# Triangle multiplication and a Fourier layer on one Trainium2 core: transposed sides kept one step apart, and the transform's sums moved to ScalarE's queue with two buffers

## The chip, the cores and the metric

The kernel runs on one core of one Trainium2 chip, as a single program. The metric is device time in microseconds. Of the kernel before there are three timed runs: 1973.91, 1974.03 and 1977.88 us, so the median is 1974.03 us. The engines have short names in what follows: PE is TensorE (matmuls and transposes), DVE is VectorE, ACT is ScalarE, POOL is GpSimd, and SP is SyncE, which only starts transfers. An engine followed by q (SPq, ACTq) means the transfers that this engine starts.

## The reference, cut to what matters

The input is one image of 512 × 512 positions with 64 channels, float32. Two layers follow each other, and each is added to its input.

```python
# layer 0: triangle multiplication on the group-normed input
xn = layernorm(gn(x))
left  = (xn @ left_w  + left_b)  * mask * sigmoid(xn @ lgate_w + lgate_b)
right = (xn @ right_w + right_b) * mask * sigmoid(xn @ rgate_w + rgate_b)
out_gate = sigmoid(xn @ ogate_w + ogate_b)
out = einsum('bkjd,bkid->bijd', left, right)       # per channel a 512 x 512 x 512 product
x = x + (layernorm(out) @ out_w + out_b) * out_gate

# layer 1: spectral convolution on the group-normed result
x_ft = fft2(gn(x))[..., :12, :12]                  # 12 x 12 modes are kept
x = x + real(ifft2(einsum('bcmn,comn->bomn', x_ft, w_real + 1j * w_imag)))
```

The mask is the product of a 0/1 vector over rows with the same over columns, so whole rows and columns of left and right are zero. Only the rows whose mask is 1 take part in the product.

## The kernel before, in words

The program counts the rows whose mask is 1 and takes a compact branch when there are at most 256, which is the case measured. There the triangle's sides are 256 × 256 for each of the 64 channels. The output rows without the mask get the bias of the output projection alone in the place of the triangle's result.

Four stages follow each other: the group norm's statistics and the gathering of the masked rows (0 to some 225 us), the projections to left and right (to some 440 us, written to the tensors `left_d` and `right_d` in device memory), the joint stage (to some 1660 us), and the inverse transform with the output (to 1973 us). The change lies in the joint stage.

The joint stage is one software-pipelined loop over steps `s`; a unit `k` has 8 steps, and `n` is the step within the unit. A unit is 256 rows by 32 columns of the image, and holds two blocks of 128 rows. There are 40 units: units 0 to 13 are rows without the mask (half 1) of the first 14 column groups, units 14 to 21 are the rows of the triangle's products (LayerNorm and output projection, stored to `u_d`), unit 22 (called `first`) and unit 39 (called `last`) are the two remaining groups without the mask, and units 23 to 38 are the masked rows (half 0) of all 16 column groups. All engines get their instructions in the order of the Python loop: it runs under a manual schedule, so the order inside a step is the order on each engine.

What the steps do, by the names in the code:

- **Sides** (`load_side`, `turn_side`, `keep_side`). Each of the 128 sides (64 channels, left and right) is loaded by SP into one of four `loose` buffers, transposed by PE (L1147) into `side_ps`, of which there is one PSUM buffer, and copied to one of four `turned_sides`. A left side is copied half by DVE (L1158) and half by ACT (L1159). A right side is copied and masked by two ACT operations (L1156).
- **Triangle** (`triangle`, `masked`). Each half of a channel's product is two matmuls on PE (L1167) into one half of the single PSUM tile `tri_pair`. DVE masks it one step later (L1174) into `staged`; after the second half SP stores the channel to `tri_d`. `halves` gives the steps of the 128 halves: two in each of the 12 steps before step 0, then 104 of them spread over steps 0 to 93, so most steps there hold one and a few hold two.
- **Rows of the image** (`transpose`, `centered`, `squared`, `summed`, `root`). PE transposes the rows (L992), multiplies them by the centring weights (`y_ps`, L1015, in the first units together with the gate's weights; `c_ps`, L999, from unit 22 on), ACT squares the result (L1035), DVE sums the squares (L1046), and once a unit, at n = 5, ACT takes the root (L1052).
- **Gate** (`gated`, `added`, `load_u`). The projection is scaled on DVE (L1333, L1339), passed through the sigmoid on ACT (L1275), multiplied on POOL by the triangle's result `u` (L1074) and added on POOL to the image rows (L1078). Four quarters `c` of a unit follow each other in this way, each of them over two steps. In units 23 to 38 the rows of `u` come through `load_u`: 32 transfers on SP (L1065), one for each of 32 columns, whose row number is read from registers that SP loads first (L646). Even quarters need the transfers 0 to 15, odd ones 16 to 31. There are two buffers for `u`.
- **Transform** (`transform`, `save`, `fetch`, `columns`). At n = 0 and n = 4 of the following unit, PE multiplies the two row blocks of a finished unit by the row basis (L1108) into `f_ps`. At n = 5 ACT copies it (L1119) into the buffer `ft`, and four transfers of 48 KB (L1133) take it to `modes_d`. Seven of the eight transfers that fetch these sums back, 768 KB in most cases, go over SP at n = 6 of certain units (L903) and one over ACT; PE multiplies what was fetched by the column basis (`columns`, L893), and DVE adds it to `sums` (L897).
- **Stores of rows** (`store`). SP stores each finished row block to `x1_h` (L1094), the first at n = 7 of the unit and the second at n = 3 of the next.

The order inside a step of the loop is this: transposes of later rows, `masked` of the half that the step before left, the projection, `centered`, `transform`, then for each half `triangle` and the transposes `turn_next` of the side two halves later, then on ACT the sigmoid, `root`, `squared`, then `keep_next` of the side just transposed, `save`, POOL's `gated` or `added`, and DVE's statistics, sums and scaling. Line numbers in this text are those of the kernel before.

## Time and profile before

The numbers are of one profiled execution, with its own time beside its span.

| | value |
|---|---|
| median of three runs | 1974.03 us (1973.91 to 1977.88) |
| profiled execution, its own time | 1974.68 us |
| its span, from first to last instruction | 1972.9 us |
| mean granted clock of TensorE in it | 0.852 |
| PE busy | 1588.0 us, 80% of the span |
| PE weight loads busy | 1217.3 us, 62% |
| DVE busy | 1412.6 us, 72% |
| ACT busy | 1018.8 us, 52% |
| POOL busy | 935.3 us, 47% |
| traffic | 524.41 MB, 266 GB/s over the span |

The page's shares are means over stages that have different limits, so a reader should not add up savings of them. Some lines of the profile give a start, a duration, an engine and a line of the code, then the operation, what it writes and reads and how many it groups, and in brackets how long the engine sat idle before it and what ended that. A list of waits gives, for an engine and a line, what it waited for: the total, how many times, and the longest, in microseconds. Matmuls are pipelined, so that the spans of neighbouring groups on PE overlap.

### The profile page before, as it was taken

How to read it: one execution, taken by the hardware profiler on the slowest of the kernel's cores; microseconds unless marked ns; L12 is line 12 of the kernel's file. 1: busy time of each engine (PE TensorE's matmuls, PEld its weight loads, DVE VectorE, ACT ScalarE, POOL GpSimd, SP SyncE). 2: the span in 40 equal slices, each digit the busy share in tenths (PEclk: the TensorE clock that was granted, in tenths of full speed). 3: DMA queues.
4: the chain of work that ended last, by engine and by line, in shares of the span. 5: the costliest groups of instructions: out<-in, count | busy, mean ns of one | idle time of the engine just before them, and what ended most of it. 6: DMA issues, size and time to landing. Idle time of an engine off the chain costs nothing. (4 is left out here: it accounts for less than half of the span.)

```text
span 1972.9 us, 33265 instructions
## 1 busy us (share of the span) xinstructions
PE 1588.0 (80%) x11014; PEld 1217.3 (62%) x11014; DVE 1412.6 (72%) x2988; ACT 1018.8 (52%) x1853; POOL 935.3 (47%) x695
## 2 busy tenths in 40 slices
PE   6788899976887778877868798788869866998773
PEld 6676666625766656656647697777768753665441
DVE  7989688872467666767798688677768766775552
ACT  3565666643676666656766576565655642111000
POOL 4665111101165455555577688677776756121110
PEclk9989999997999898989879899888989886555555
DMA  7998388877566656656469976776777679999999
GB/s 296 385 386 318 84 240 227 235 235 259 165 226 197 207 184 215 218 186 221 155 170 309 319 251 221 231 233 216 240 256 231 223 226 355 424 427 426 427 427 386
DMA packets 229956, 524.41 MB, mean 266 GB/s; under 512 B 49968, under 2 KB 165936, under 8 KB 188816
## 3 DMA queue, kind: packets, MB, share of 16 engines
q1 hardware_dynamic: 193472, 301.55, 45.1%
q0 software_dynamic: 32832, 218.45, 30.6%
q10 hardware_dynamic: 3472, 2.20, 0.4%
q8 instruction: 90, 1.47, 0.3%
q14 instruction: 90, 0.74, 0.1%
HBM read 314.55 MB, written 207.55 MB: 265 GB/s over the span
## 5 line engine op out<-in xcount | busy, mean ns | idle before, releaser
L1078 POOL TENSOR_TENSOR places<-places,z_t 128x1024 f32<-128x1024 f32 x127 | 299.9, 2362 | 8.2
L1074 POOL TENSOR_TENSOR z_t<-z_t,bias_row_out 128x1024 f32<-128x1024 f32 x63 | 148.7, 2361 | 296.2 <-ACT z_t L1275 194.4
L1503 PE MATMUL l_ps<-places,rinv 24*128 24x512 f32 x512 | 208.2, 1116 | 31.4 <-DVE places L1510 20.1
L1184 DVE BATCH_NORM_STATS2 stats2c<-places 128x6 f32<-128x128 f32 x1024 | 220.5, 279 | 13.4 <-POOL places L1078 13.3
L1046 DVE TENSOR_REDUCE scratch<-sq_c 128x16 f32<-128x1024 f32 x160 | 194.7, 1217 | 47.5 <-ACT sq_c L1035 33.8
L1167 PE MATMUL tri_c_ps<-places 128*128 128x256 f32 x512 | 154.5, 428 | 77.5 <-DVE places L1174 74.2
L1074 POOL TENSOR_TENSOR z_t<-z_t,places 128x1024 f32<-128x1024 f32 x64 | 151.1, 2362 | 115.6 <-ACT z_t L1275 55.7
L999 PE MATMUL c_ps<-center_x,xt_c 128*128 128x128 f32 x1152 | 164.4, 289 | 44.6 <-ACT xt_c L994 43.9
L1503 PEld LDWEIGHTS l_ps<-places,rinv 24*128 24x128 f32 x512 | 120.2, 301 | 114.3 <-DVE places L1510 61.0
L999 PEld LDWEIGHTS c_ps<-center_x,xt_c 128*128 128x128 f32 x1152 | 150.4, 204 | 47.7 <-ACT xt_c L994 46.8
L992 PE MATMUL t_ps<-c_ident,places 128*128 128x128 f32 x1024 | 170.5, 294 | 6.6 <-DMA places<-in_x,src_i 6.6
L999 PE MATMUL w_ps<-gate_x,xt_c 128*128 128x128 f32 x1152 | 166.7, 292 | 11.1 <-DVE z_t L1333 10.7
L1275 ACT ACTIVATE z_t<-z_t 128x1024 f32<-128x1024 f32 x128 | 135.3, 1058 | 67.2 <-DVE z_t L1339 66.0
L1167 PEld LDWEIGHTS tri_c_ps<-places 128*128 128x128 f32 x512 | 92.6, 201 | 119.4 <-DVE places L1174 85.6
L999 PEld LDWEIGHTS w_ps<-gate_x,xt_c 128*128 128x128 f32 x1152 | 152.7, 207 | 18.7 <-DVE z_t L1333 18.7
L1339 DVE TENSOR_TENSOR z_t<-z_t,scratch 128x1024 f32<-128x1024 f32 x128 | 156.3, 1221 | 9.2 <-ACT rs_n L1052 4.0
L688 DVE BATCH_NORM_STATS2 stats1c<-x_ps 128x6 f32<-128x512 f32 x256 | 156.3, 686 | 8.1 <-PE x_ps L687 7.8
L1158 DVE COPY places<-side_ps 128x256 f32<-128x256 f32 x64 | 27.2, 425 | 181.1 <-PE side_ps L1147 181.1
L992 PEld LDWEIGHTS t_ps<-c_ident,places 128*128 128x128 f32 x1024 | 131.8, 154 | 34.6 <-issue 34.0
L1015 PE MATMUL y_ps<-both,xt_y 64*128 64x128 f32 x1792 | 136.2, 294 | 19.8 <-ACT xt_c L1042 19.6
L1510 DVE TENSOR_TENSOR places<-places,l_ps 128x512 f32<-128x512 f32 x176 | 110.5, 683 | 56.5 <-DMA places<-x_h,dst_i 47.4
L1015 PEld LDWEIGHTS y_ps<-both,xt_y 64*128 64x128 f32 x1792 | 114.4, 196 | 42.2 <-ACT xt_c L1042 28.8
(219 smaller groups left out, 3160.4 us busy)
## 6 DMA issues: line engine op xcount, KB each, us to landing
x_h<-places SPq DMA_DIRECT2D x64, 1024.0 KB
out_x<-places SPq DMA_DIRECT2D x44, 1024.0 KB
places<-u_d SPq DMA_DIRECT2D x512, 64.0 KB
out_x<-lx_t SPq DMA_DIRECT2D x20, 1024.0 KB
rbc<-rs_d POOLq DMA_DIRECT2D x32, 512.0 KB, 7.6
left_d<-o_c SPq DMA_DIRECT2D x64, 256.0 KB
right_d<-o_c SPq DMA_DIRECT2D x64, 256.0 KB
places<-left_d SPq DMA_DIRECT2D x64, 256.0 KB
```

The lines of the kernel that those rows point to most:

```text
L688: nc.vector.bn_stats(stats[:, 0, 16 * (jc % quarter) + 4 * r + c, :], ps.rearrange("p i k -> p (i k)"))
L992: nc.tensor.transpose(tps[:, i, :], flat[:, o : o + P], ident)
L999: nc.tensor.matmul(ps[:, 2 * i : 2 * i + 2, :], xts[s][:, i, :], w, start=True, stop=True)
L1015: nc.tensor.matmul(ps[:, h, i, :], of[hs, i, :], both[hs], start=True, stop=True)
L1046: nc.vector.tensor_reduce(totals[k % 2][:, 8 * (n - 1) : 8 * (n + 1)], sqs.pop(s // 2), AX.X, ALU.add)
L1074: nc.gpsimd.tensor_mul(zs[k, c], zs[k, c], u)
L1078: nc.gpsimd.tensor_add(xr, xr, zs.pop((k, c)))
L1167: nc.tensor.matmul(tri_of[h], lt[:, kb, b * P : (b + 1) * P], rt[:, kb, :], start=(kb == 0), stop=(kb == 1))
L1184: nc.vector.bn_stats(st[nth[k] // 4][:, g, nth[k] % 4, :], x_of(k)[:, :, 2 * g : 2 * g + 2])
L1275: nc.scalar.activation(zs[k - i, c], zs[k - i, c], AF.Sigmoid)
L1339: nc.vector.tensor_add(z, z, bias_ps["ogate"].unsqueeze(1).to_broadcast([P, 16, C]))
L1503: nc.tensor.matmul(ps.rearrange("p j o -> p (j o)"), rinv[h, b, :], it[h], start=True, stop=True, tile_position=(32 * g, 0),)
```

## The change

Five edits are made in the joint stage.

1. `save` has two places for `ft` that alternate with `k`, but for the last units, and its four transfers are always started by ACT. In before SP started them but for one unit.
2. `fetch` is always started by ACT.
3. The side that is transposed in a step is now kept (copied out of PSUM) at the start of the next step, and it is the side three halves ahead and not two. `triangle` of a step's first half moves ahead of the projection and `centered`; the transposes come after `centered`. Where a step has two halves, the first is followed by its transposes and their copy at once. Before the first half three sides are transposed. The loads of sides follow the transposes, and so come one half earlier.
4. Up to unit 21, `transform` moves ahead of `centered`, and `root` of units up to 21 moves behind `squared`.
5. `load_u` moves from n = 2 to n = 3 of a unit, behind the second store of the unit before.

```diff
                 def fetch(half, h):
-                    (nc.scalar if (half, h) == (0, 3) else nc.sync).dma_start(modes_t[:q], modes_d[half][h * P : h * P + q])
+                    nc.scalar.dma_start(modes_t[:q], modes_d[half][h * P : h * P + q])
...
-                        ft = places[:, 7 * 64 * C + M2 * C : 7 * 64 * C + 32 * C].rearrange("p (j c) -> p j c", c=C)
+                        o = 7 * 64 * C + (M2 * C if k % 2 == 1 or k > last - 4 else 32 * C)
+                        ft = places[:, o : o + 8 * C].rearrange("p (j c) -> p j c", c=C)
                         nc.scalar.copy(ft.rearrange("p j c -> p (j c)"), fs.pop(k))
...
-                            queue = nc.scalar if (jc, half) == (NJ - 2, 0) else nc.sync
-                            queue.dma_start(modes_d[half][o : o + 8].rearrange("j m c -> m j c"), ft[32 * g : 32 * g + M2])
+                            nc.scalar.dma_start(modes_d[half][o : o + 8].rearrange("j m c -> m j c"), ft[32 * g : 32 * g + M2])
...
+                    turned_now = []
+
                     def turn_next(g):
                         if g < 2 * C:
                             turn_side(g)
+                            turned_now.append(g)
                             if g + 4 < 2 * C:
                                 load_side(g + 4)
 
-                    def keep_next(g):
-                        if g < 2 * C:
-                            keep_side(g)
+                    def keep_next():
+                        if turned_now:
+                            keep_side(turned_now.pop())
...
+                        if s == begin:
+                            for g in range(3):
+                                turn_next(g)
+                                if g < 2:
+                                    keep_next()
+                        keep_next()
                         if s + LEAD < total_g:
                             transpose(s + LEAD)
                         for h in unmasked:
                             masked(h)
                         unmasked = []
-                        if s == begin:
-                            for g in range(2):
-                                turn_next(g)
-                                keep_next(g)
+                        for h in mine[:1]:
+                            triangle(h)
+                            if len(mine) > 1:
+                                turn_next(h + 3)
+                                keep_next()
...
+                        if n in (0, 4) and held(k - 1) and k < first:
+                            transform(k - 1, n // 4)
                         if 0 <= s + LEAD - 1 < total_g:
                             cps = centered(s + LEAD - 1)
-                        if n in (0, 4) and held(k - 1):
+                        if n in (0, 4) and held(k - 1) and k >= first:
                             transform(k - 1, n // 4)
-                        for h in mine:
+                        for h in mine[1:]:
                             triangle(h)
-                            turn_next(h + 2)
-                            if h != mine[-1]:
-                                keep_next(h + 2)
+                        for h in mine[-1:]:
+                            turn_next(h + 3)
...
-                        if n == 5 and 0 <= k + 1 < len(units):
+                        if n == 5 and first <= k + 1 < len(units):
                             root(k + 1)
                         if cps is not None:
                             squared(s + LEAD - 1, cps)
-                        if mine:
-                            keep_next(mine[-1] + 2)
+                        if n == 5 and 0 <= k + 1 < first:
+                            root(k + 1)
                         if n == 5 and held(k - 1):
                             save(k - 1)
...
-                        if n == 2 and first < k < last - 1:
+                        if n == 3 and first < k < last - 1:
                             load_u(k - first)
```

## The prediction

> **What bounds the kernel now.** I read the page's slices first: the last six (from about 1660 us) have DMA at 9 tenths, so the inverse transform is bound by transfers and cannot gain from this change. The change lives in the joint stage, 440 to 1660 us. The table of windows splits it (columns: PE, PEld, DVE, ACT, POOL busy us, PEclk, DMA share, GB/s):
>
> ```profile
> 558.00:960.00 402.00, 319.24 (x2588) 251.64 (x2586) 275.83 (x640) 260.68 (x470) 214.63 (x103) 0.93 0.62 205
> 1212.00:1618.00 406.00, 329.88 (x2524) 297.81 (x2524) 301.59 (x703) 233.62 (x340) 292.21 (x140) 0.87 0.71 230
> ```
>
> No engine is full in either, so waits decide. The first window holds the triangle beside units 1 to 11; its list of waits (total us, times, longest) shows a ring from PE to DVE and back:
>
> ```profile
> DVE places L1158 <- PE side_ps L1147: 145.1, 56, 6.5
> PE tri_c_ps L1167 <- DVE places L1174: 72.1, 47, 3.9
> ACT places L1156 <- PE side_ps L1147: 61.1, 25, 6.9
> ACT places L1159 <- DVE places L1158: 54.7, 44, 3.1
> ```
>
> The timeline of PE and then DVE at one place shows how it turns:
>
> ```profile
> 671.21 1.16 PE L1015 MATMUL y_ps<-both,xt_y 64*128 64x128 f32 x16
> 674.46 2.08 PE L1167 MATMUL tri_c_ps<-places 128*128 128x256 f32 x4 [2.08 <-DVE places L1174]
> 679.07 1.13 PE L1167 MATMUL tri_c_ps<-places 128*128 128x256 f32 x4
> 680.04 0.60 PE L1147 MATMUL side_ps<-c_ident,places 128*128 128x128 f32 x4
> 676.94 0.48 DVE L1174 SCALAR_TENSOR_TENSOR places<-tri_c_ps,slot_t,mask_s 128x256 f32<-128x256 f32 x1
> 680.68 0.42 DVE L1158 COPY places<-side_ps 128x256 f32<-128x256 f32 x1 [3.26 <-PE side_ps L1147]
> ```
>
> DVE sits 3.26 us in front of a copy of 0.42 because the transposes stand behind the product and the rest of PE's step. After PE's gap the same product takes 2.08 instead of 1.13 us. Pairs of steps take 9.8 us here (671.2 to 681.0). Saves of sums (ACT L1119) start at 581.36 in unit 1 and 973.59 in unit 11: 39.2 us a unit.
>
> In the second window (units 24 to 38, 29.0 us each by the saves at 1211.93 and 1617.67), the waits and SP's timeline say:
>
> ```profile
> ACT places L1119 <- DMA modes_d<-places: 71.7, 13, 7.2
> PE t_ps L893 <- DMA places<-modes_d: 31.4, 4, 8.8
> POOL z_t L1074 <- DMA places<-u_d: 32.6, 13, 5.1
> ```
>
> ```profile
> 1301.92 18.28 SPq L1065 DMA_DIRECT2D places<-u_d  x32
> 1320.31 0.36 SPq L1094 DMA_DIRECT2D x_h<-places  x1
> 1320.77 3.94 SPq L1133 DMA_DIRECT2D modes_d<-places  x4
> 1324.81 0.35 SPq L1094 DMA_DIRECT2D x_h<-places  x1
> 1329.18 0.91 SPq L1065 DMA_DIRECT2D places<-u_d  x2
> ```
>
> SP repeats after 27.3 us (1301.92 to 1329.18): 18.3 for 32 loads of u, 3.9 for four stores, 0.7 for two stores of rows, and 4 us for the row numbers' registers before the next set. It is the limit, and POOL is close behind: eight operations of 2.37 us and two gathers of about 1.0, 21 of the 29.
>
> **The change part by part.** The sum goes against the profiled execution, 1974.68 us (span 1972.9); the median of the runs is 0.65 lower.
>
> *Sides kept a step apart, transform and root moved, first stage.* What goes is the wait of the copies for side_ps. What is late next is the ring product, `masked`, product: there is still one tri_pair tile. In a step with a left side DVE's order is keep, `masked`, and PE's is product 1.13, y 1.16, turn 0.60, so the ring is 1.13 + 1.16 + 0.60 + 0.42 + 0.48 = 3.8 us; with a right side the keeping is ACT's and PE's own work decides, 1.13 + 1.16 + 0.60 and 0.3 for transposes of rows (L992, 294 ns in the page) = 3.2. A pair is 7.0, four pairs 28.0; two transforms at 1.07 (1345.07, below) make 2.1, the one step per unit with two halves some 1.3: 31.4. To that comes ACT at n = 5 and 6, where nothing waits for it now but sides to be kept: a table load of 1.28 for the root, the copy 0.59, and four issues:
>
> ```profile
> 1617.67 0.59 ACT L1119 COPY places<-f_ps 128x512 f32<-128x512 f32 x1 [4.40 <-issue]
> 1618.28 2.06 ACTq L1133 DMA_DIRECT2D modes_d<-places  x4
> 1620.43 1.28 ACT L1275 ACT_TABLE_LOAD   x1 [2.18 <-DVE stats2c L1184]
> ```
>
> These are the kernel's only four stores that ACT issues already, 2.06 us; with one table load and the copy not hidden some 4.5 us a unit. So 35.9 for 39.2, times 11 units: **-36**. Ends: below, PE's busy time alone, 319.24/402 of 39.2 at clock 0.93, is 28.9 at full clock: -113. Above, pairs stay at 9.8 and ACT's 2.1 us come on top: +23. Unit 0 and the first double steps (PE holds them) get nothing.
>
> *Products stage, saves 12 to 14.* ACT's stores queue there beside `load_product` on SP: **+5**, between 0 and +12 (three saves at 2.1 to 4).
>
> *Stores and fetches off SP, two buffers, u loads one step later.* Removed: 3.94 us of SP per unit, seven fetches (some 0.35 each, as an issue of rows), and ACT's wait of 71.7 us in front of L1119. SP alone would then need 23.0 us a unit. But the changed program's list of waits shows what comes in. The transfers of SP and ACT take eight completion semaphores in turn, and each waits until the one eight places before it has landed. In before, SP's own order made that harmless. Now ACT's four stores of unit k-1's sums are placed among the 32 loads of u that unit k needs: in units 29, 31, ... 37 after loads 8, 12, 15 and 18 (counted from 0), so that load 15 waits for store 1 to land; in units 30, 32, ... 36 after 6, 9, 12 and 15, so that load 19 waits for store 3, which waits for store 1. SP stands there with 17 or 13 loads to issue. That closes a ring that was open: POOL's last `added` of k-1, transform, copy, store, rest of the u loads, `gated`(k, 1) and on to the last `added` of k. Its parts:
>
> - copy 0.59, issue 0.52 (a quarter of 2.06): 1.1;
> - landing of a store, from the trace's landing events, median 3.3 in this stage (1.4 to 7.2; 6.4 to 7.1 for ACT's four at 1618);
> - 17 loads at 18.28/32 = 0.57: 9.7; in the other units a second issue and landing (3.8) and 13 loads, 7.4;
> - landing of the last load, 3.0 (1.7 median of all, 3.5 the longest usual);
> - POOL: six operations and a gather, 15.5, by these rows:
>
> ```profile
> 1338.34 2.38 POOL L1078 TENSOR_TENSOR places<-places,z_t 128x1024 f32<-128x1024 f32 x1
> 1340.71 2.37 POOL L1074 TENSOR_TENSOR z_t<-z_t,places 128x1024 f32<-128x1024 f32 x1
> 1343.22 0.98 POOL L638 DMA_INDIRECT places<-in_x,src_i  x1
> 1345.07 1.07 PE L1108 MATMUL f_ps<-places,hb 128*32 128x512 f32 x8
> 1353.54 0.58 ACT L1119 COPY places<-f_ps 128x512 f32<-128x512 f32 x1 [3.48 <-DMA modes_d<-places]
> ```
>
> - transform to copy: 1345.07 to 1353.54 less the wait of 3.48, 5.0.
>
> Together 37.6 and 39.1 us, where 29.3 stand now (saves at 1353.54 and 1617.67, nine units: 264.1). Nine units are 5 × 37.6 + 4 × 39.1 = 344.4: **+80**. Units 27 and 28, with stores behind loads 15 to 25 and 7 to 16, have 34.3 and 38.8 for 27.9 and 26.0: **+19**. Units 24 to 26 hang on late loads only: 0. In unit 38 the stores sit behind loads 3 to 13; from its save to POOL's next unit 36 instead of 14.7: **+21**. Unit 23 is freed of SP's stores: -3. Sum +117. With the shortest landings (1.4, 1.7) the ring is 33, sum +45; with 7 for stores it is 41 to 47, +190. The waits removed, 71.7 and 31.4, lie inside the ring and are no gain beside it: once the ring binds, ACT and PE wait longer for other things.
>
> One rule would speak otherwise. The Trainium skill, "DMA: Bandwidth & Descriptors", section "Issuing engines are not separate DMA queues", says that spreading issues over engines saves sequencer time only, since the transfers share the 16 DMA engines. SP's row agrees that issuing is the limit here; by the rule alone 14 units would save SP's 4.3 us each, -60. It says nothing of ordering between queues, and no run here shows that yet.
>
> Inverse stage: nothing. Sum: -36 + 5 + 117 = +86: 2060.7 by the profiled execution, 2060 by the median.
>
> **The rivals.**
> *SP's relief decides* (the other side, and the change doing what it says). If stores land before SP reaches the loads behind them, a unit falls from 29.0 to SP's 23.0: 14 × -6.0 = -84, with -36 earlier about 1855. For it: the copy's wait and SP's full row are real. Against it: the stores can't be issued before POOL has finished unit k-1, and the loads behind them are wanted by POOL straight after. It decides from the point where the ring is shorter than 29.0 us; its POOL part and 17 loads alone are 25.
> *The triangle gains in full.* If ACT's extra 4.5 us hide, -86 there, and 2010 in all. For it: ACT has 35% idle in the first window. Against it: sides now need ACT in every step.
> *ACT becomes a bound as well.* While store 3 waits for store 1, all of ACT's squares, sigmoids and xt_c stand behind it, some 7 us; with no gain in the triangle and the ring near its upper end, 2120 to 2170. For it: ACT is in order and feeds PE. Against it: ACT is busy 16.7 us a unit of 39.
>
> **How the numbers follow.** Forecast 0.70 (2025 to 2110, likeliest 2060), triangle in full 0.12 (1985 to 2025), ACT bound 0.09, SP's relief 0.09. A difference within 0.2% (4 us) can't be told from no change. Faster 0.10 (SP's relief and the low end of the ring), same 0.02, slower 0.88. The range, 1988 to 2130, leaves out SP's relief and the far ends of the others.
>
> **What would show it.** Right: saves of ACT 37 to 40 us apart in units 29 to 38; SP idle inside its sets of loads, waiting for modes_d; POOL's L1074 waiting for u_d much longer than 32.6 us; ACT's waits between its four stores; saves of units 1 to 11 about 36 us apart, with L1158 hardly waiting. Wrong: saves 23 to 28 us apart in the main stage with SP's loads unbroken, or units 1 to 11 at 39 or more.

## The result, and the profile after

The changed kernel takes 2099.82 us (median of four runs, 2097.86 to 2101.50), where the kernel before took 1973.98 us in the same sessions: a ratio of 1.063, 95% interval 1.061 to 1.065. It is slower by 126 us. The forecast was 2060 us with a range of 1988 to 2130. The profiled execution after has a span of 2096.1 us against 1972.9, so the two traces differ by 123.2 us, close enough to the medians to look for the loss in the traces. In the lines of the changed kernel the copy of the sums is L1120, the scaling L1344 and L1350, the sigmoid L1286; the others kept their numbers.

The saves of the sums (ACT's copy, once a unit) cut the joint stage into pieces. All times are differences between starts of that copy; the save in unit k is called save k.

| stretch | before | after | difference | forecast |
|---|---|---|---|---|
| start of the program to save 1 | 581.4 | 600.3 | +19.0 | 0 |
| saves 1 to 11 (triangle beside ten units) | 392.2 | 406.0 | +13.8 | -33 |
| saves 11 to 23 (end of triangle, products) | 209.7 | 214.5 | +4.8 | +2 |
| saves 23 to 24 | 28.6 | 23.0 | -5.6 | -3 |
| saves 24 to 27 | 87.7 | 86.1 | -1.6 | 0 |
| saves 27 to 29 | 53.9 | 67.1 | +13.1 | +19 |
| saves 29 to 38 (nine units) | 264.1 | 328.2 | +64.1 | +80 |
| save 38 to the last one | 32.1 | 48.0 | +15.9 | +21 |
| last save to the end of the span | 323.1 | 322.7 | -0.3 | 0 |

(The forecast's -36 were for eleven units, 3.3 each; +2 is its +5 less the eleventh of them.) The differences add up to 123.2. So 86 us of the loss lie behind save 23, and 38 us ahead of it, where the forecast had a gain.

The table of windows after (the columns are window, its length, then PE, PEld, DVE, ACT and POOL busy, PE's clock, DMA share and GB/s), the first of the same place as before, the second from save 24 on:

```profile
558.00:960.00 402.00, 319.76 (x2472) 239.46 (x2470) 268.13 (x610) 254.82 (x457) 208.68 (x101) 0.89 0.60 198
1243.00:1725.00 482.00, 345.07 (x2532) 290.07 (x2530) 305.62 (x706) 231.79 (x341) 285.14 (x137) 0.87 0.58 191
```

In the second window POOL does 285 us of work as before (292 in 406), but takes 482 us for it. In the first, fewer instructions fit into the same 402 us on every engine, and PE's clock is 0.89 instead of 0.93.

**Units 29 to 38.** SP's waits from 1390 to 1730 us, then its timeline in one stretch:

```profile
SPq L1065 <- DMA modes_d<-places: 106.5, 10, 11.8
SPq L1065 <- DMA places<-u_d: 11.5, 11, 1.8
SPq L1094 <- DMA places<-u_d: 3.3, 3, 1.3
```

```profile
1379.82 30.20 SPq L1065 DMA_DIRECT2D places<-u_d  x32
1410.13 1.37 SPq L1094 DMA_DIRECT2D x_h<-places  x2
1417.35 2.94 SPq L1065 DMA_DIRECT2D places<-u_d  x6
```

SP's loads of u stand ten times, 10.6 us each, for a store of the sums to land, though no byte of a load depends on a store. A set of 32 loads takes 30.2 us where it took 18.28. SP has no store of sums left to issue, and all that it gained is lost inside its sets. POOL feels it: its waits from 1243 to 1700 us are led by

```profile
POOL z_t L1074 <- DMA places<-u_d: 165.8, 23, 14.4
```

for 32.6 us in the prediction's list of before, which ends at 1600 us. One turn of the ring, unit 29, from the timelines of ACT, POOL and PE:

```profile
1397.07 0.59 ACT L1120 COPY places<-f_ps 128x512 f32<-128x512 f32 x1
1397.69 4.06 ACTq L1133 DMA_DIRECT2D modes_d<-places  x4
1401.79 0.69 ACT L994 ACTIVATE xt_c<-t_ps,ab_xc 128x512 f32<-128x512 f32 x1 [4.13 <-DMA modes_d<-places]
1403.41 2.38 POOL L1074 TENSOR_TENSOR z_t<-z_t,places 128x1024 f32<-128x1024 f32 x1 [13.54 <-DMA places<-u_d]
1413.41 2.34 POOL L1074 TENSOR_TENSOR z_t<-z_t,places 128x1024 f32<-128x1024 f32 x1 [4.13 <-DMA places<-u_d]
1426.53 2.35 POOL L1078 TENSOR_TENSOR places<-places,z_t 128x1024 f32<-128x1024 f32 x1
1429.59 1.06 PE L1108 MATMUL f_ps<-places,hb 128*32 128x512 f32 x8
1435.85 0.59 ACT L1120 COPY places<-f_ps 128x512 f32<-128x512 f32 x1
```

ACT copies at 1397.07. By the trace's landing events the first store is issued by 1397.99 and lands at 1401.26; SP issues load 15 at 1401.28 and load 31 by 1410.02; that one lands at 1412.99. POOL's `gated` of the second quarter starts at 1413.41, the last `added` ends at 1428.88, the transform follows, and the next copy starts 38.8 us after the first. In each unit from 29 to 37 SP idles 10 to 12 us in front of one load of its set, load 15 in the odd units and load 19 in the even ones, as the prediction had placed them.

**Units 1 to 11.** The waits from 500 to 960 us (the prediction's list of the first window is of this stretch too):

```profile
ACT sq_c L1041 <- PE y_ps L1015: 101.0, 80, 5.3
PE tri_c_ps L1167 <- DVE places L1174: 90.6, 64, 4.5
DVE places L1158 <- PE side_ps L1147: 56.6, 36, 3.4
DVE z_t L1344 <- ACT rs_n L1052: 45.1, 10, 5.9
ACT places L1159 <- DVE places L1158: 33.0, 21, 3.3
ACT places L1156 <- PE side_ps L1147: 12.8, 14, 1.1
```

The wait that the change was about fell from 145.1 to 56.6 us, and ACT's from 61.1 to 12.8. Away from n = 5 a pair of steps takes 6.7 us on PE (first to second line), for 9.8 before and 7.0 in the forecast:

```profile
824.73 1.13 PE L1167 MATMUL tri_c_ps<-places 128*128 128x256 f32 x4 [2.35 <-DVE places L1174]
831.47 1.13 PE L1167 MATMUL tri_c_ps<-places 128*128 128x256 f32 x4 [0.47 <-DVE places L1174]
```

But there is a new wait: DVE in front of its scaling for ACT's root, 45.1 us in ten units. The place of it in unit 6:

```profile
796.78 0.60 ACT L1041 ACTIVATE sq_c<-y_ps 128x512 f32<-128x512 f32 x1 [0.61 <-PE y_ps L1015]
797.87 1.28 ACT L1052 ACT_TABLE_LOAD   x1
799.16 0.31 ACT L1052 ACTIVATE rs_n<-scratch,eps 128x64 f32<-128x64 f32 x1
799.51 0.69 DVE L1344 TENSOR_TENSOR z_t<-xt_c,scratch 128x512 f32<-128x512 f32 x1 [5.26 <-ACT rs_n L1052]
802.23 2.08 PE L1167 MATMUL tri_c_ps<-places 128*128 128x256 f32 x4 [4.51 <-DVE places L1174]
```

The root now stands behind the squares, which wait for PE's y. The scaling uses other columns than the root, but both read the one PSUM tile `scratch`, and in the program's list of waits L1344 waits for the root ahead of it. `masked` (L1174) stands behind the scaling on DVE, and the next product waits for `masked`: PE idles 4.51 us, and then takes 2.08 us for a product that took 1.13 in the rows above. The granted clock is 0.50 there (the table of windows again):

```profile
802.00:804.00 2.00, 1.77 (x4) 1.18 (x4) 2.00 (x6) 1.68 (x3) 0.00 (x0) 0.50 0.85 224
```

That the shared tile is the reason of the wait is inferred; no run gives the two their own tiles.

### The profile page after: what moved, and what is told of

Read it like the earlier page. It is cut to its first block, busy times and chain, and to the rows that moved or that the text cites. A ratio compares the mean times of both kernels' runs of the same rounds, so it can differ in the third digit from the quotient of the medians.

```text
span 2096.1 us, 33114 instructions
## 1 busy us (share of the span) xinstructions
PE 1626.5 (78%) x11014; PEld 1212.9 (58%) x11014; DVE 1412.6 (67%) x2988; ACT 1021.5 (49%) x1853; POOL 935.2 (45%) x695
## 3 DMA queue, kind: packets, MB, share of 16 engines
q0 software_dynamic: 32832, 218.45, 28.5%
## 5 line engine op out<-in xcount | busy, mean ns | idle before, releaser
L1344 DVE TENSOR_TENSOR z_t<-w_ps,rs_n 128x512 f32<-128x512 f32 x144 | 97.4, 676 | 157.1 <-PE w_ps L999 147.8
L1108 PE MATMUL f_ps<-places,hb 128*32 128x512 f32 x512 | 104.4, 696 | 113.1 <-POOL places L1078 112.1
L994 ACT ACTIVATE xt_c<-t_ps,ab_xc 128x512 f32<-128x512 f32 x144 | 98.8, 686 | 181.3 <-PE t_ps L992 129.8
L999 PE MATMUL w_ps<-gate_x,xt_c 128*128 128x128 f32 x1152 | 168.4, 294 | 14.1 <-DVE z_t L1344 13.8
L999 PEld LDWEIGHTS c_ps<-center_x,xt_c 128*128 128x128 f32 x1152 | 147.0, 200 | 41.5 <-ACT xt_c L994 40.6
L1286 ACT ACTIVATE z_t<-z_t 128x1024 f32<-128x1024 f32 x128 | 136.0, 1062 | 70.4 <-DVE z_t L1350 70.1
L999 PEld LDWEIGHTS w_ps<-gate_x,xt_c 128*128 128x128 f32 x1152 | 154.9, 209 | 22.4 <-DVE z_t L1344 20.5
L1015 PEld LDWEIGHTS y_ps<-both,xt_y 64*128 64x128 f32 x1792 | 126.7, 214 | 61.6 <-issue 23.3
L1350 DVE TENSOR_TENSOR z_t<-z_t,scratch 128x1024 f32<-128x1024 f32 x128 | 156.3, 1221 | 6.6 <-ACT rs_n L1052 0.9
L1015 PE MATMUL y_ps<-both,xt_y 64*128 64x128 f32 x1792 | 150.0, 314 | 9.5 <-ACT xt_c L1042 9.5
```

Source lines behind the costliest of these rows:

```text
L999: nc.tensor.matmul(ps[:, 2 * i : 2 * i + 2, :], xts[s][:, i, :], w, start=True, stop=True)
L1015: nc.tensor.matmul(ps[:, h, i, :], of[hs, i, :], both[hs], start=True, stop=True)
L1286: nc.scalar.activation(zs[k - i, c], zs[k - i, c], AF.Sigmoid)
L1350: nc.vector.tensor_add(z, z, bias_ps["ogate"].unsqueeze(1).to_broadcast([P, 16, C]))
```

## The experiments

The theory at the start was: behind save 23 the ring through the turn of completion semaphores makes the loss; ahead of it the new order of the steps does, by the late root and by the first product of the double steps. The rivals were ACT's own time at its issues, the fetches, and the turning of three sides at the start. In the diffs below the base is the changed kernel, unless another is named. Each run stood beside runs of the kernel before on the same chip.

### The queue part alone

```diff
 (kernel before, sides as they were)
-                    (nc.scalar if (half, h) == (0, 3) else nc.sync).dma_start(modes_t[:q], ...)
+                    nc.scalar.dma_start(modes_t[:q], ...)
+                        o = 7 * 64 * C + (M2 * C if k % 2 == 1 or k > last - 4 else 32 * C)
...
+                            nc.scalar.dma_start(modes_d[half][o : o + 8]...)
...
-                        if n == 2 and first < k < last - 1:
+                        if n == 3 and first < k < last - 1:
```

> The kernel before with the queue part alone: stores and fetches of the sums started by ACT, two buffers for ft, loads of u one step later; the sides as before. If the ring of stores and loads through the shared completion semaphores makes the loss, units 23 to 39 lose here what they lose in the changed kernel (from save 23 to the last save 552 us for 466, +86) and the triangle stage loses at most ACT's four issues, 0 to 25 us: 2060 to 2085 us. The rival, that the loss comes from sides and transform in other places on PE and ACT, gives at most the 1974 of before, and by SP's relief alone about 1890.

Measured: 2094.78 us, ratio 1.061 (1.059 to 1.063), 119 us above the kernel before. From save 23 to the last save it takes 546.2 us (466.5 before, 552.4 in the changed kernel), from save 1 to 11 it takes 420.5 (392.2 before). The ring is there without any change to the sides, with the same wait of SP, here from 1243 to 1718 us:

```profile
SPq L1065 <- DMA modes_d<-places: 111.9, 11, 10.9
```

The time is above the expected 2060 to 2085, because the queue part costs 28 us in ten units ahead of save 11, and not 0 to 25. Half of that shows in the lists of waits from 500 to 960 us, where PE's y waits longer for ACT's copy of an earlier projection; the first line is of the kernel before, the second of this run:

```profile
PE y_ps L1015 <- ACT xt_c L1042: 14.2, 16, 1.8
PE y_ps L1015 <- ACT xt_c L1042: 28.0, 18, 4.8
```

What makes the other half was not traced.

### The sides alone

```diff
-                    nc.scalar.dma_start(modes_t[:q], ...)
+                    (nc.scalar if (half, h) == (0, 3) else nc.sync).dma_start(modes_t[:q], ...)
...
 (stores by SP, one ft, load_u at n == 2, as in the kernel before)
```

> The changed kernel with the queue part undone: sides a step apart, transform and root moved, but stores and fetches by SP, one buffer, loads of u at n = 2. In the changed kernel the first twelve double steps and unit 0 lose 19 us and units 1 to 11 lose 14. Theory: both losses belong to the new order of the steps (PE waits for the masked half, DVE waits for the late root), so they stay here, less ACT's issues: 1985 to 2010 us. Rival: they come from the four issues of ACT in each save, 2.3 us each time, and the new order itself gains: 1935 to 1965.

Measured: 2018.57 us, ratio 1.023 (1.020 to 1.027). It loses 24.5 us up to save 1 (605.9), 8.6 from save 1 to 11 (400.8), 9.0 from there to save 23, and gains 4.8 behind it. So the rival falls: without a single store on ACT the new order loses. The time is 9 us above the range; DVE's wait for the root is 43.5 us here, as in the changed kernel.

### The root ahead of the squares again

```diff
 (the sides alone)
-                        if n == 5 and first <= k + 1 < len(units):
+                        if n == 5 and 0 <= k + 1 < len(units):
                             root(k + 1)
                         if cps is not None:
                             squared(s + LEAD - 1, cps)
-                        if n == 5 and 0 <= k + 1 < first:
-                            root(k + 1)
```

> As the run with the sides alone, but the root stands before the squares again, as in the kernel before. Theory: DVE's scaling (L1344) waits 5 us a unit for the root, which stands behind two squares and a table load; with the root ahead of them 13 units gain 4 to 5 us, so 50 to 65 us less than the sides alone: 1930 to 1955. Rival: that wait is only where DVE would wait for PE anyhow; then within 10 us of the sides alone.

Measured: 1964.59 us, ratio 0.995 (0.994 to 0.997): 54 us less than the run above, inside the expected 50 to 65, and 0.5% faster than the kernel before. The expected time of 1930 to 1955 was missed all the same, since the run above had come out 9 us over its own range. Saves 1 to 11 take 365.4 us, 36.5 a unit, where the forecast had 35.9. The wait has shrunk to

```profile
DVE z_t L1342 <- ACT rs_n L1052: 12.0, 6, 3.6
```

One line of the change, the root's place, thus cost more than the sides' new order gained.

### Stores by SP from unit 22 on

```diff
-                            nc.scalar.dma_start(modes_d[half][o : o + 8]..., ft[32 * g : 32 * g + M2])
+                            queue = nc.scalar if k < first or (jc, half) == (NJ - 2, 0) else nc.sync
+                            queue.dma_start(modes_d[half][o : o + 8]..., ft[32 * g : 32 * g + M2])
```

> The changed kernel, but from unit 22 on SP starts the stores of the sums again (two buffers, fetches on ACT and the later loads of u stay). Theory of the ring: it is gone, SP's loads run through in 18 us, units take 27 to 29 us as before: 86 to 115 us less than the changed kernel, 1985 to 2014. Rival: the loss in units 23 to 39 comes from the fetches on ACT, the two buffers or the later loads; then it stays above 2070.

Measured: 2016.52 us, ratio 1.020 (1.018 to 1.023), 83 us less than the changed kernel, and 2.5 us above the expected 1985 to 2014. From save 23 to the last save it takes 463.3 us. The fetches on ACT, the two buffers and the later loads stayed, so they are not the loss. SP's waits, from 1255 to 1662 us, no longer have a load that waits for a store (L1134 is the store's line here):

```profile
SPq L1134 <- DMA places<-u_d: 13.0, 19, 1.3
SPq L1065 <- DMA places<-u_d: 3.4, 4, 1.1
```

It also shows what the two buffers are worth with SP as it was, together with the fetches on ACT and the later loads: 463 us for 466. ACT's wait of 71.7 us ahead of its copy, the longest in the list of before, is 7.4 us here, and its going gained next to nothing.

### The first product of a double step behind the projection

```diff
 (sides alone, early root)
-                        for h in mine[:1]:
-                            triangle(h)
-                            if len(mine) > 1:
-                                turn_next(h + 3)
-                                keep_next()
+                        if len(mine) == 1:
+                            triangle(mine[0])
...
+                        if len(mine) > 1:
+                            triangle(mine[0])
+                            turn_next(mine[0] + 3)
+                            keep_next()
+                            triangle(mine[1])
```

> As the run with the early root, but in steps with two halves the first product stands behind the projection again, as before (product, transposes, keep, product, transposes). Theory: in the first twelve double steps PE waits 0.5 and 1.55 us in turn for the masked half of the step before, 5.6 us a step for 4.65; with y in between that wait is covered: 11 us less there and some 3 us less in the later double steps, 1948 to 1954. Rival: the late first save (600.9 against 581.4) comes from the three sides turned at the start; then no more than 3 us change.

Measured: 1954.43 us, ratio 0.990 (0.986 to 0.993), 10 us less than the early root alone, and just above the expected range. The first save comes at 591.2 and not at 600.9. PE's products and projections in the changed kernel, and then in this run:

```profile
484.26 1.13 PE L1167 MATMUL tri_c_ps<-places 128*128 128x256 f32 x4 [1.56 <-DVE places L1174]
486.85 1.13 PE L1167 MATMUL tri_c_ps<-places 128*128 128x256 f32 x4
489.33 1.13 PE L1167 MATMUL tri_c_ps<-places 128*128 128x256 f32 x4 [0.47 <-DVE places L1174]
495.47 1.13 PE L1167 MATMUL tri_c_ps<-places 128*128 128x256 f32 x4 [1.55 <-DVE places L1174]
```

```profile
486.93 1.13 PE L1167 MATMUL tri_c_ps<-places 128*128 128x256 f32 x4
491.60 1.13 PE L1167 MATMUL tri_c_ps<-places 128*128 128x256 f32 x4
496.46 1.13 PE L1167 MATMUL tri_c_ps<-places 128*128 128x256 f32 x4
```

Two double steps take 11.2 us in the changed kernel (484.26 to 495.47), with PE waiting for the masked half, and 9.5 here (486.93 to 496.46) with no wait. The 24 halves of the first twelve double steps take 60.8 us here, 68.3 with the early root alone and 59.6 in the kernel before (from the first product to the one behind the 24). So half of the late first save is explained by this. Most of the other half (591.2 against 581.4) is the rival of the expectation, the third side turned at the start. Here PE waits for that side's load ahead of its first product, while in the kernel before it turned the side behind that product (the line of this run, then of the kernel before, whose first product starts at 464.50):

```profile
468.26 1.09 PE L1147 MATMUL side_ps<-c_ident,places 128*128 128x128 f32 x4 [4.83 <-DMA places<-left_d]
467.61 0.63 PE L1147 MATMUL side_ps<-c_ident,places 128*128 128x128 f32 x4 [1.21 <-DMA places<-left_d]
```

From the first transposition of a side to the first product it takes 15.7 us here and 8.8 before, 6.9 of the 9.8 us. No run turns two sides there in the new order.

### Transform behind the projection

```diff
 (the run above)
-                        if n in (0, 4) and held(k - 1) and k < first:
-                            transform(k - 1, n // 4)
                         if 0 <= s + LEAD - 1 < total_g:
                             cps = centered(s + LEAD - 1)
-                        if n in (0, 4) and held(k - 1) and k >= first:
+                        if n in (0, 4) and held(k - 1):
```

> As the run before in this list, and transform stands behind centered everywhere, as before. Theory: it moves 1.07 us of PE work within the step twice a unit, ahead of or behind y, on which ACT waits in every step; behind is at least as good for ACT: within 10 us of the run before. A rival says that the transform ahead of centered was needed to hide masked; then 1 us in each of 28 steps, up to 28 us slower.

Measured: 1950.10 us, ratio 0.987 (0.983 to 0.990). The interval overlaps that of the run above (0.986 to 0.993), so this part of the change made no difference that these runs can tell.

### Stores by POOL from unit 22 on

```diff
-                            nc.scalar.dma_start(modes_d[half][o : o + 8]..., ft[32 * g : 32 * g + M2])
+                            to, src = modes_d[half][o : o + 8]..., ft[32 * g : 32 * g + M2]
+                            if k < first:
+                                nc.scalar.dma_start(to, src)
+                            elif (jc, half) == (NJ - 2, 0):
+                                nc.scalar.dma_start(to, src)
+                            else:
+                                put_off.append((to, src))
...
+                        if n == 7:
+                            for to, src in put_off:
+                                nc.gpsimd.dma_start(to, src)
+                            put_off.clear()
```

> The changed kernel, but from unit 22 on POOL starts the four stores of a unit's sums, at n = 7; POOL's transfers take other completion semaphores than those of SP and ACT. This opens the ring and leaves SP relieved. Theory: SP needs 23.4 us a unit, POOL 21 and four issues of 0.55 to 0.6 (its row for a direct transfer), so units take 24 to 26 us instead of 36.5: 1940 to 1975. Rival: SP's issues are not what holds 29 us a unit in the kernel before; then no less than 2005, as with the stores on SP.

Measured: 2008.54 us, ratio 1.017 (1.010 to 1.024). From save 23 to the last save it takes 456.8 us. The ring is open and SP is relieved, as its timeline and, for POOL's issues, POOL's show:

```profile
1397.26 18.28 SPq L1065 DMA_DIRECT2D places<-u_d  x32
1415.65 1.11 SPq L1094 DMA_DIRECT2D x_h<-places  x2
1422.95 18.09 SPq L1065 DMA_DIRECT2D places<-u_d  x32
1401.02 2.64 POOL L1368 DMA_DIRECT2D modes_d<-places  x4
```

A set takes 18 us again and they follow each other after 25.7 us. Some units take 24.0 us, as expected, but the mean of saves 29 to 38 is 28.5, and the last group, whose stores ACT still issued, has 42 us for 32. In all it is 91 us less than the changed kernel, but from save 23 to the last save only 10 us less than before. The time is not the theory's 1940 to 1975; it lies where the rival put it, above 2005. So SP's full row in the profile of before was not a limit worth 84 us, as one rival of the prediction had it. What follows close behind, this trace shows in part, from 1345 to 1605 us (the table of windows, then POOL's longest wait):

```profile
1345.00:1605.00 260.00, 223.87 (x1709) 186.02 (x1709) 201.30 (x469) 154.35 (x229) 220.05 (x132) 0.97 0.72 238
POOL z_t L1074 <- DMA places<-u_d: 29.8, 7, 5.1
```

POOL is busy 220 of the 260 us, 24 us a unit, and waits for u in 30 of the 40 that are left. Five of the seven waits, 20 us, end with loads of u that SP issued while a gather of POOL was on its way (the last section has more on these). No run moves the gathers, so this is a reading and not a test.

### ACT's stores later in the turn

```diff
-                            nc.scalar.dma_start(modes_d[half][o : o + 8]..., ft[32 * g : 32 * g + M2])
+                            to, src = modes_d[half][o : o + 8]..., ft[32 * g : 32 * g + M2]
+                            if k < first or (jc, half) == (NJ - 2, 0):
+                                nc.scalar.dma_start(to, src)
+                            else:
+                                put_off.append((to, src))
...
+                        if n == 1:
+                            for to, src in put_off:
+                                nc.scalar.dma_start(to, src)
+                            put_off.clear()
```

> The changed kernel, but from unit 22 on ACT starts the same four stores at n = 1 of the next unit and not at n = 5 (but for the last group, save 38). Engine, count and size of the transfers stay; what changes is their place among SP's loads in the turn of completion semaphores: behind load 31 of the set and not behind loads 6 to 18. If it is the ring through the loads that costs 86 us in units 23 to 39, SP's sets run through in 18 us, and units 27 to 37 take 24 to 29 us for 36.5: 1990 to 2020 us. If the loss is ACT's own time at its issues or the fetches on ACT, the time stays above 2070.

Measured: 2057.66 us, ratio 1.041 (1.037 to 1.045): 42 us less than the changed kernel, and neither expectation held. From save 23 to the last save it takes 501.9 us for 552.4. The units from save 29 to 38 take 31.2 us for 36.5. The ring was not opened but moved. SP's waits from 1390 to 1700 us, and one place in SP's and ACT's timelines:

```profile
SPq L1065 <- DMA modes_d<-places: 63.1, 12, 7.8
```

```profile
1418.35 1.90 SPq L1065 DMA_DIRECT2D places<-u_d  x4
1422.07 2.05 ACTq L1366 DMA_DIRECT2D modes_d<-places  x4
1424.93 15.34 SPq L1065 DMA_DIRECT2D places<-u_d  x28
```

Behind load 31 of one set, the stores are ahead of the next set: its load 4 waits for the first of them, issued at 1422.07 and landed at 1424.91. I had reckoned that they would have landed long before. That the place in the turn alone, with engine, number and size of the transfers kept, moves nine units by 47 us still speaks for the ring, and against ACT's own time at its issues: from the first to the last of the four ACT takes 1.7 us on average here and 2.9 in units 29 to 37 of the changed kernel, waits between them included, which is 1.2 of the 5.2 us a unit.

### ACT's issues beside the new order

```diff
 (stores by SP from unit 22 on)
-                        if n == 5 and first <= k + 1 < len(units):
+                        if n == 5 and 0 <= k + 1 < len(units):
...
-                        if n == 5 and 0 <= k + 1 < first:
-                            root(k + 1)
```

> Sides a step apart with the early root; stores on ACT up to unit 21 (two buffers) and on SP from unit 22 on; fetches on ACT, loads of u at n = 3. Against the run with the early root (stores on SP, 365 us from save 1 to save 11) this shows what ACT's four issues cost beside the new order: by the prediction's terms 2.1 us a unit, so 386 us from save 1 to save 11 and 1985 to 1990 in all. Rival: with the late root away, they hide in ACT's slack: 365 to 370 and 1960 to 1968.

Measured: 1966.86 us, ratio 0.996 (0.994 to 0.998). Saves 1 to 11 take 372.9 us, 7.5 more than with the stores on SP, so 0.75 us a unit and not 2.1. That is just above the rival's 365 to 370 us and far from 386, and the time is the rival's: in the new order most of ACT's issues are hidden. The 0.75 comes from one trace of each kernel; the medians of the timed runs differ by only 2.3 us. Why more is hidden than in the old order is not shown.

### The gains together

The first run has the early root and the late double steps, the stores of the triangle stage on SP with two buffers, and POOL's stores from unit 22 on.

> Sides a step apart with the early root and the late double steps, stores of the triangle stage on SP with two buffers, stores from unit 22 on POOL, fetches on ACT, loads of u at n = 3. Theory: the gains add: 1948 to 1954 for the first part, less 40 to 70 for the ring open and SP relieved: 1880 to 1914. If SP's relief is worth nothing, 1945 to 1960.

Measured: 1939.02 us, ratio 0.982 (0.978 to 0.986). Saves 1 to 11 take 363.4 us, and 450.1 from save 23 to the last. The gain of the sides is there in full, that of the open ring and the relieved SP is 16 us and not 40 to 70; with POOL's stores alone it was 10. The time lies between the two expectations, nearer to the one in which SP's relief is worth nothing.

The second has ACT's stores at n = 1 of the next unit in the place of POOL's, the last group too, and transform behind the projection.

> Sides a step apart, root early, transform behind centered, double steps late; stores up to unit 21 on SP with two buffers; from unit 22 on ACT's stores at n = 1 of the next unit, the last group too; fetches on ACT. Theory: 1950 as measured for the first part, less what an open ring and a relieved SP give beside POOL's 21 us, 24 to 28 us a unit for 29.0: 1890 to 1935. If ACT's issues cost there what SP saves, 1945 to 1960.

Measured: 1990.37 us, ratio 1.008 (1.006 to 1.011). The sides' gain is kept (360.2 us from save 1 to 11), and the moved ring takes it away again (503.3 us from save 23). Neither expectation held, for the reason found above.

The third is the first with POOL's stores in the last group too, and transform behind the projection.

```diff
-                            elif (jc, half) == (NJ - 2, 0):
-                                nc.scalar.dma_start(to, src)
                             else:
                                 put_off.append((to, src))
```

> As the run with the sides and POOL's stores, but POOL starts the stores of the last group (save 38) too, and transform stands behind centered everywhere. Theory: in that run the last group alone still had ACT's stores within the turn of SP's loads; POOL waited 9.75 us for u there and from save 38 to the last save it took 42 us, where the kernel before takes 32. That goes, and transform's place gives 0 to 4 us as measured: 1939 less 10 to 14, 1925 to 1930 us. Rival: the 10 us come from the end of the stage itself (gathers for the inverse on POOL); then 1935 to 1940.

Measured: 1934.25 us, ratio 0.978 (0.976 to 0.981), the lowest median of all, though its interval overlaps that of the first of these three. The theory's 1925 to 1930 was missed. From save 38 to the last save it takes 39.8 us, not 32: of the 10 us the theory expected, 2 came. What holds the last group is left open.

## Why the prediction was right or wrong

**The ring: right.** The direction and most of the size came from it. Forecast +117, measured +86 behind save 23. It was found in the list of waits of the changed program, against what SP's full row and ACT's longest wait suggested. Its terms, in unit 29: copy and issue 0.92 (forecast 1.1), landing of the first store 3.27 (3.3), loads 15 to 31 in 8.76 (9.7), landing of the last 2.97 (3.0), start of `gated` 0.4 (not in the sum), POOL 15.47 (15.5), transform to copy 6.97 (5.0). Together 38.8 for 37.6. The odd units from 29 to 37 take 37.0 us on average, but that is close in part by luck. Unit 29 is the exception in the store's landing: in units 31, 33, 35 and 37 the first store lands 1.4 us after its issue, and not 3.3. What makes up for it is the end of the turn: from the landing of the last load to the next copy it is 22.6 to 22.9 us in units 29 to 36, for 20.5 in the sum (20.0 in unit 37). The sum's short end, 33 us, does not follow from its own terms, which give 34.4 and 34.0.

**The even units: mis-sized.** They were to be slower, 39.1, for a second store that waits for the first. They take 35.8. The first store lands 1.4 to 2.4 us after its issue, and the third 1.35 after its own: 3.3 us together on average, where the sum had 6.6. The last load lands after 1.6 us for 3.0, and the end of the turn takes 2.2 us more than in the sum. So the landings were mis-sized: the median of the stage before the change was taken for stores that land sooner in the changed kernel. Why they do is not shown. The 3.3 us in each of four even units, and 0.6 in each of five odd ones, are the 16 us between 80 and 64.

**Triangle, 36 us gained: wrong.** The step that failed is "ACT at n = 5 and 6 ... some 4.5 us a unit". It priced ACT's own instructions, and took the root's move behind the squares for one of position. Nobody was asked who waits for the root. The answer was in the waits of the changed program: the scaling on DVE, `masked` behind that, and the product behind `masked`; 4.5 us a unit on DVE, and PE's lower clock behind it (0.50 after the wait shown). Units 1 to 11 took 40.6 us each, beyond the 39 that the prediction had named as a sign of being wrong. With the root back, the unit is 36.5 us without ACT's issues and 37.3 with them, for 35.9 in the sum. The ring product, `masked`, product was sized well (a pair 7.0, measured 6.7). That the whole unit comes near 35.9 says less: the parts named for ACT, 1.28, 0.59 and 2.06, add up to 3.9 and not 4.5, and most of the 2.06 was hidden, so other parts of the unit took more than the sum had.

**ACT's four issues at 2.1 us: a term that depends on the order.** By the traces the queue part costs 0.75 us a unit in the new order and 2.8 in the old. The parts of the change therefore do not add: 119 us for the queue part alone and 43 for the sides alone, 126 together.

**"Unit 0 and the first double steps ... get nothing": wrong.** They lost 19 us. The first product of a double step was moved ahead of the projection, and so directly behind `masked` on which it depends; the projection had covered that wait. In the trace of the changed kernel the 24 halves of these steps take 12.3 us more (71.9 for 59.6), and the stretch from there to save 1 takes 8.5 more (65.8 for 57.3); of the latter, 6.9 went in the run that moved only the root. The third side at the start puts the first product 3.2 us further behind the first transposition (12.0 for 8.8). The first transposition itself came 5.0 us earlier in this trace; it lies between 450.7 and 459.6 us in the runs, so that single traces compare there only to a few us. With the old place of the product and the early root, the double steps are back at 60.8.

**Products stage, +5: near in size**, by the run with the queue part alone, which takes 5.3 us more than before from save 11 to 23. The sides alone take 9.0 more there and both together 4.8, so that the agreement in the changed kernel is no proof of the term. The inverse stage did not move (-0.3).

**The rivals.** SP's relief does not decide: with the ring open and SP relieved, units 23 to 39 gain 10 to 17 us, not 84. The page of the Trainium skill that the prediction weighed ("DMA: Bandwidth & Descriptors", "Issuing engines are not separate DMA queues") says that starting transfers on several engines saves sequencer time only. No more than that came: those 10 to 17 us, of the 60 that the prediction had worked out for it. A gain in the triangle exists (27 to 33 us from save 1 to 11 in the runs with the early root and SP's stores) but needs the root where it was, and not even there is it the rival's 86. ACT as a bound was not seen: it is busy 232 us in 482, and its four issues take 2.4 to 4.1 us a unit from 27 on, waits between them included.

In the traces the sum was 37 us too low (86 against 123): ahead of save 23 it was 69 us too low (-31 against +38), behind it 31 too high. The total came out near because the two errors have opposite signs, and that is luck: the mechanism behind save 23 was right, the gain ahead of it was not.

## What to carry to other kernels

Before a transfer is moved to another engine's queue, list with what it shares completion semaphores, in which order, and what stands behind it in that order: a late store in the middle of early loads makes the loads wait for the computation that the store belongs to. Where an instruction is moved on an engine that is not busy, ask who waits for its result, also by a shared tile, and not what it costs on its engine. And where two edits are made together, price each beside the other: an issue that was in the way in the old order was hidden in the new one.

## What the runs showed of the hardware that was not expected

Loads of u that SP issues while one of POOL's gathers is on its way land late. In unit 29 of the changed kernel POOL issues a gather from 1405.93 to 1406.91 us, and it lands at 1411.78. The load issued by 1405.74 us lands after 1.7 us and the one by 1406.78 after 2.0; the load issued by 1407.29 lands after 4.7, and the five behind it land one after the other until 1412.99. By the landing events of the whole trace, the 151 loads issued between the end of a gather's issue and its landing take 4.05 us in the median, and 356 others 1.59; with POOL's stores it is 4.08 (151 loads) and 1.60 (349). That the loads queue behind the gathers' packets is likely but was not tested.
